# Attention transposes moved from TensorE to VectorE and SBUF-to-SBUF DMAs

## The chip, the cores and the metric

The kernel runs on one core of one Trainium2 chip. A core has a matrix engine (TensorE, PE in the profile, with its weight loads listed as PEld), a vector engine (VectorE, DVE), a scalar engine (ScalarE, ACT), a general engine (GpSimd, POOL), and SyncE (SP), which here only issues DMAs. Each engine works through its own instruction list in order; a DMA is issued from the list of SP, ACT or POOL and then runs on 16 shared DMA engines. Work is held in SBUF, and TensorE writes its results to PSUM, which has eight banks; both have 128 partitions.

The metric is the device time of one execution in microseconds. The time before is the median of three runs.

## The reference

Everything is float32. The input x has 4 batch elements of 512 rows and 1024 columns. It is layer-normed, goes through an attention branch s and a gate branch g, and the output is x + s * g.

```
xn = layernorm(x)                                # 4 x 512 x 1024
q = rmsnorm(xn @ Wq.T, q_norm_w)                 # 32 heads of 128
k = rmsnorm(xn @ Wk.T, k_norm_w)                 # 8 KV heads of 128
v = xn @ Wv.T                                    # 8 KV heads of 128
scores = q @ k.T / sqrt(128)                     # 4 query heads share a KV head
bias = where(rel > 0, -1e30, slope[head] * rel)  # rel = key position - query position
s = (softmax(scores + bias) @ v) @ Wo.T
g = silu(xn @ W.T + bias + lora(xn))             # 8 adapters of rank 16, averaged with weights
out = x + s * g
```

The mask is causal: a query looks only at keys at or before its own position.

## The kernel before

The kernel has three stages. The first layer-norms x, turns it so that its 1024 columns lie on the partitions, stores it to DRAM as the seven left operands of a Strassen product, and computes half of the gate. The last multiplies by Wo and adds everything up. The change is in the middle stage, which computes attention.

The middle stage goes through 32 units. A unit is one KV head with its four query heads (`g`, 8 values) and one batch element (`b`, 4 values, the inner loop). For each unit `project_qkv` computes queries, keys and values, 128 rows by 768 columns a tile, by two Strassen halves of seven products each (`strassen`, L118). A product is four matmuls of 384 columns (L125). Its left operand `a` is loaded from DRAM by SP just ahead of it (L384) into one of eight buffers. Banks of PSUM are saved by ScalarE (L214) and added up by VectorE (L221, L223) into the tiles `c`, one for each 128 rows. Then `norm` takes a finished tile: POOL copies v out (L398), ScalarE squares queries and keys (L400), VectorE reduces (L402) and scales (L404), POOL takes the power -1/2 (L406), VectorE multiplies (L408). `transposes` turns the 128x128 blocks of four query heads and one key head on TensorE (L420, L425), and VectorE copies them out of PSUM with the norm weights applied (L421, L426).

`attend` goes through the unit's 16 items, a head `h` and a block `i` of 128 queries. `scores` makes one tile of 128 queries by (i+1)*128 keys (L445). VectorE adds the slope times the relative position, with the mask in it (L452), and finds the negated maximum of each row (L461). ScalarE takes the exponential with its row sum (L464), VectorE forms the reciprocal (L468) and scales the row (L469). `turn` transposes the probabilities on TensorE, i+1 blocks of 128x128 (L478), and ScalarE copies them to `pt` (L479). `values` multiplies with v for one head (L487), ScalarE copies the result (L495) and issues four DMAs to DRAM (L497).

PSUM: three banks hold products, two scores, two transposes, one values.

The unit loop (L555 to L561) takes one step of the next unit's projection after each step of `attend`, so that the products stand between the score tiles on TensorE. In the last unit half of the gate for batch element 0 stands in for the projection; its products have 256 columns. The order written in the loop is not the final one: a scheduler places the instructions of each engine by its own estimates of when operands are ready, with the tile pools' buffers as limits. What counts for an engine is its final list.

## Time and profile before

The columns of the table are busy times of one profiled execution.

| | us |
|---|---|
| median of three runs (3116.28 to 3120.14) | 3118.26 |
| span of the profiled execution, first to last instruction | 3112.8 |
| device time of the profiled execution | not listed beside its span |
| TensorE busy in the span | 2969.5 (95%) |
| VectorE busy | 1622.0 (52%) |
| ScalarE busy | 835.7 (27%) |
| GpSimd busy | 560.8 (18%) |
| matmuls of the score tiles (L445) | 360.0 |
| matmuls that transpose probabilities (L478) | 225.5 |
| matmuls of values (L487) | 300.6 |
| matmuls that transpose queries and keys (L420, L425) | 81.3 and 35.8 |

One float32 matmul stands as two records in the profile. The mean duration of a group is that of single records, which overlap on TensorE; the time that a matmul holds the engine is seen better in the start times of the timeline. A row of the cost groups gives the line, engine and operation, what is written and read, the count, then busy time and mean, then the idle time just before them and what ended it. In the rows of DMA issues the last number is the median time from issue to landing.

### The profile page before, as it was taken

To read this page: it belongs to the slowest core of one execution; us is meant where nothing else is said; L and a number is where in the kernel's file an instruction comes from. 1 tells how busy PE (TensorE), PEld (TensorE's weight loads), DVE (VectorE), ACT (ScalarE), POOL (GpSimd) and SP (SyncE) were. 2 spreads that over 40 slices of the span, in tenths; PEclk is the share of its full clock that TensorE was granted. 3 is DMA by queue.
4 is the path that set the end of the run, shared out by engine and by line. 5 is a ranking of instruction groups with operands and counts; after the bars stand their busy time and mean duration, and the time that the engine had idled before them with its cause. 6 is when DMAs were issued, how large, how long until landed. Compare 5 with 4: busy or idle time off the path is not lost.

```text
span 3112.8 us, 30258 instructions
## 1 busy us (share of the span) xinstructions
PE 2969.5 (95%) x10408; PEld 1754.6 (56%) x10408; DVE 1622.0 (52%) x3474; ACT 835.7 (27%) x2132; POOL 560.8 (18%) x513
## 2 busy tenths in 40 slices
PE   7999999999999999999999999999979999999997
PEld 5766566655656556655665565656844444344443
DVE  5236665666565665666566656566332232322564
ACT  1123333333333333333333333333200000000010
POOL 5321200121020120121012102012020121311311
PEclk9999999999999999999999999999999999999999
DMA  8532332232232232233223223222662244443364
GB/s 307 206 122 78 95 89 78 78 112 75 78 113 77 75 113 78 78 90 97 78 78 112 74 78 102 75 75 82 198 230 81 108 142 138 159 142 132 134 220 148
DMA packets 201769, 360.12 MB, mean 116 GB/s; under 512 B 21520, under 2 KB 95248, under 8 KB 199056
## 3 DMA queue, kind: packets, MB, share of 16 engines
q1 hardware_dynamic: 114272, 265.86, 27.4%
q10 hardware_dynamic: 75568, 50.37, 5.1%
q0 software_dynamic: 11776, 41.95, 3.3%
q8 instruction: 84, 1.38, 0.2%
q14 instruction: 69, 0.57, 0.1%
HBM read 265.82 MB, written 92.27 MB: 115 GB/s over the span
## 4 chain that ended last, share of the span: by engine, by line
PE 82%; DVE 9%; POOL 4%; issue 2%; DMA 2%; ACT 1%; ACTq 0%; POOLq 0%; SPq 0%; DVEq 0%
PE c_p L125 20%; PE u_p L125 14%; PE c_o L125 13%; PE u_o L125 10%; PE sc L445 8%; PE ov L487 7%; PE ptp L478 4%; PE c_f L125 3%; POOL inv L406 2%; PE u_f L125 2%; PE tq L420 2%; DVE qn L408 1%; DVE pr L469 1%; DVE ss L402 1%; DVE sc L452 1%
## 5 line engine op out<-in xcount | busy, mean ns | idle before, releaser
L445 PE MATMUL sc<-kT,qT 128*128 128x128 f32 (+3 forms) x1024 | 360.0, 437 | 12.9 <-ACT pr L464 12.5
L464 ACT ACTIVATE pr<-sc,nmax 128x128 f32<-128x128 f32 (+3 forms) x512 | 269.8, 527 | 379.2 <-DVE nmax L461 321.7
L125 PE MATMUL c_p<-w,a 128*128 128x384 f32 x1024 | 361.8, 487 | 0.0
L479 ACT COPY pt<-ptp 128x128 f32<-128x128 f32 (+3 forms) x512 | 216.0, 422 | 532.0 <-PE ptp L478 527.5
L125 PE MATMUL u_p<-t_q,a 128*128 128x384 f32 x1024 | 351.6, 487 | 0.0
L125 PE MATMUL c_p<-t_q,a 128*128 128x384 f32 x1024 | 351.5, 487 | 0.0
L452 DVE SCALAR_TENSOR_TENSOR sc<-rel,sc 128x128 f32<-128x128 f32 (+3 forms) x512 | 251.5, 491 | 152.3 <-PE sc L445 145.1
L487 PE MATMUL ov<-pt,v 128*128 128x512 f32 (+3 forms) x1024 | 300.6, 433 | 0.0
L398 POOL COPY v<-c_p 128x128 f32<-128x128 f32 x128 | 37.8, 295 | 1358.8 <-DVE c_p L221 1116.1
L445 PEld LDWEIGHTS sc<-kT,qT 128*128 128x128 f32 x1024 | 182.0, 191 | 131.7 <-ACT pr L464 36.9
L461 DVE TENSOR_REDUCE nmax<-sc 128x1 f32<-128x128 f32 (+3 forms) x512 | 249.4, 487 | 11.0
L125 PE MATMUL u_o<-t_o,s 128*128 128x512 f32 x512 | 237.3, 608 | 18.2 <-DVE k_o L642 17.3
L650 DVE TENSOR_TENSOR c<-c_o,k_o 128x512 f32<-128x512 f32 x96 | 66.2, 690 | 361.4 <-ACT k_o L640 191.0
L487 PEld LDWEIGHTS ov<-pt,v 128*128 128x128 f32 x1024 | 187.3, 191 | 115.6 <-issue 50.6
L125 PEld LDWEIGHTS u_p<-t_q,a 128*128 128x128 f32 x1024 | 185.1, 191 | 107.8 <-issue 5.5
L469 DVE TENSOR_SCALAR pr<-pr,rden 128x128 f32<-128x128 f32 (+3 forms) x512 | 236.5, 462 | 13.4
L125 PEld LDWEIGHTS c_p<-t_q,a 128*128 128x128 f32 x1024 | 185.2, 191 | 102.2
L468 DVE RECIPROCAL rden<-den 128x1 f32<-128x1 f32 x512 | 83.4, 163 | 287.7 <-ACT pr L464 287.4
L478 PEld LDWEIGHTS ptp<-ident,pr 128*128 128x128 f32 x1280 | 163.0, 141 | 119.6 <-DVE qT L421 39.5
L125 PEld LDWEIGHTS c_p<-w,a 128*128 128x128 f32 x1024 | 180.5, 191 | 86.5
L478 PE MATMUL ptp<-ident,pr 128*128 128x128 f32 x1280 | 225.5, 275 | 0.0
L640 ACT COPY k_o<-u_o 128x512 f32<-128x512 f32 x48 | 28.1, 585 | 662.2 <-PE u_o L125 662.2
(110 smaller groups left out, 3645.6 us busy)
## 6 DMA issues: line engine op xcount, KB each, us to landing
a<-xs SPq DMA_DIRECT2D x448, 256.0 KB, 2.7
ot<-oh ACTq DMA_DIRECT2D x512, 64.0 KB, 1.7
o<-ot SPq DMA_DIRECT2D x64, 512.0 KB, 3.2
sums<-c POOLq DMA_DIRECT2D x48, 512.0 KB, 5.0
old<-sums SPq DMA_DIRECT2D x48, 512.0 KB, 4.0
w<-in_wq_dram SPq DMA_DIRECT2D x8, 2048.0 KB, 8.6
wo<-in_wo_dram SPq DMA_DIRECT2D x8, 2048.0 KB, 8.7
xs<-a ACTq DMA_DIRECT2D x8, 1792.0 KB, 6.7
```

The lines of the kernel that those rows point to most:

```text
L125: nc.tensor.matmul(acc, lhsT=left[k], rhs=right[k], start=start and k == 0, stop=k == nk - 1, skip_group_check=True,)
L406: nc.gpsimd.tensor_tensor(inv, ms, neg_half, ALU.pow)
L445: nc.tensor.matmul(sc[:, :w], lhsT=qT[:, h, i * P : (i + 1) * P], rhs=kT[:, :w], start=True, stop=True,)
L452: nc.vector.scalar_tensor_tensor(sc[:, :w], rel[:, S - w :], slopes[g * G + h], sc[:, :w], ALU.mult, ALU.add,)
L461: nc.vector.tensor_reduce(nmax, sc[:, :w], AX.X, ALU.max, negate=True)
L464: nc.scalar.activation(pr[:, :w], sc[:, :w], AF.Exp, bias=nmax, accum_out=den)
L468: nc.vector.reciprocal(rden, den)
L469: nc.vector.tensor_scalar(pr[:, :w], pr[:, :w], rden, None, ALU.mult)
L478: nc.tensor.transpose(tp[:, j, :], pr[:, j * P : (j + 1) * P], ident)
L479: nc.scalar.copy(pts[h][:, 0 : i + 1, i * P : (i + 1) * P], tp[:, 0 : i + 1, :])
L487: nc.tensor.matmul(ov[:, j * P :], lhsT=v[:, j, :], rhs=pt[:, j, j * P :], start=j == 0, stop=j == NT - 1,)
L650: nc.vector.tensor_tensor(dst, acc, kept, ALU.add)
```

## The change

TensorE no longer transposes anything in the middle stage. A 128x128 transpose becomes two steps: VectorE transposes each 32x32 block in its place, and DMAs from SBUF to SBUF move the blocks to the partitions where they belong.

For queries and keys, `norm` multiplies in place in `c` and transposes 128x640 elements by blocks into `flat` (one instruction a tile). When all four tiles of the unit are done, 16 DMAs on SP move `flat` to `qkT`, each from 32 partitions to 32 partitions, in pieces of 640 bytes. Both norm weights and the factor 1/sqrt(128) are joined in `w_sb` and applied to the keys alone, by one VectorE instruction (`kT`).

A score tile now holds 32 queries of all four heads, 128 rows in all, so one tile c of 16 covers 32(c+1) keys, 128 at the least. The bias of each head lies on that head's 32 partitions: a tile `bias`, 608 columns, is made once for each KV head from `rel` and `drop`, and the tile's window of it is added. The addition and the row's maximum come from one instruction, which writes the negated sum and keeps its minimum; the exponential takes scale -1. ScalarE, not VectorE, scales the rows by the reciprocal, four tiles at a time. VectorE then transposes the 32x32 blocks into `turned`, whose blocks above the diagonal are set to zero once. At the end of the unit 16 DMAs on SP move `turned` to `pt`, in pieces of 512 bytes.

`values` goes by blocks of 128 queries with all four heads in one matmul of 512 columns; it is called one unit later, while the projection after next begins. ScalarE issues one DMA for each block. PSUM: three banks for products, three for scores, two for values. `left` has six buffers in place of eight.

```
+    nc.gpsimd.tensor_scalar(drop, drop, shift, None, ALU.add)
+    nc.gpsimd.tensor_scalar(rel, drop, 0.0, slope0, ALU.min, ALU.mult)
+    nc.gpsimd.tensor_scalar(drop, drop, 0.0, MASKED, ALU.is_gt, ALU.mult)
...
-        ps_sc = front.enter_context(tc.tile_pool(name="ps_sc", bufs=2, space=PSUM))
-        ps_tp = front.enter_context(tc.tile_pool(name="ps_tp", bufs=2, space=PSUM))
-        ps_ov = front.enter_context(tc.tile_pool(name="ps_ov", bufs=1, space=PSUM))
+        ps_sc = front.enter_context(tc.tile_pool(name="ps_sc", bufs=3, space=PSUM))
...
+            turned = keep.tile([P, 4 * npairs, NT, 32], F32, name="turned")
+            for i in range(1, NT):
+                for t in range(NT - 1):
+                    c0 = 4 * (first_pair[i] + i)
+                    nc.gpsimd.memset(turned[:, c0 + t + 1 : c0 + NT, t, :], 0.0)
...
                     nc.vector.tensor_tensor(
+                        qk, qk, inv.unsqueeze(2).to_broadcast([P, G + 1, HD]), ALU.mult
+                    )
+                    nc.vector.transpose(
+                        flat[:, t], qk.rearrange("p h (a e) -> p a h e", a=4)
+                    )
+
+                yield from project(f"p_{u}", b, G + 2, stream(u, b), right, norm)
+
+                qkT = unit.tile([P, NT, 4, G + 1, 32], F32, tag="qkT", name=f"qkT_{u}", bufs=1)
+                for a in range(4):
+                    for r in range(4):
+                        nc.sync.dma_start(
+                            out=qkT[32 * a : 32 * a + 32, :, r].rearrange("p t h e -> p t (h e)"),
+                            in_=flat[32 * r : 32 * r + 32, :, a].rearrange("p t h e -> p t (h e)"),
+                        )
+                kT = unit.tile([P, 4 * NT, 32], F32, tag="kT", name=f"kT_{u}", bufs=1)
+                nc.vector.tensor_scalar(
+                    kT,
+                    qkT.rearrange("p t r h e -> p (t r) h e")[:, :, G, :],
+                    w_sb,
+                    None,
+                    ALU.mult,
+                )
...
+                def scores(i, t, den):
+                    c = 4 * i + t
+                    w = max(32 * (c + 1), P)
...
+                        lhsT=qkT[:, i, t, 0:G, :].rearrange("p h e -> p (h e)"),
...
+                    nc.vector.tensor_tensor_reduce(
+                        out=sc[:, :w],
+                        in0=sc[:, :w],
+                        in1=bias[:, at : at + w],
+                        scale=-1.0,
+                        scalar=3.0e38,
+                        op0=ALU.add,
+                        op1=ALU.min,
+                        accum_out=low,
+                    )
...
+                for i in range(NT):
+                    den = small.tile([P, NT], F32, tag="den", name=f"den_{u}_{i}")
+                    prs = []
+                    for t in range(NT):
+                        prs.append(scores(i, t, den))
+                        if t % 2:
+                            yield
+                    rden = small.tile([P, NT], F32, tag="rden", name=f"rden_{u}_{i}")
                     nc.vector.reciprocal(rden, den)
+                    for t in range(NT):
+                        c = 4 * i + t
+                        n = max(c + 1, 4)
+                        pr = prs[t][:, : 32 * n]
+                        nc.scalar.activation(pr, pr, AF.Copy, scale=rden[:, t : t + 1])
+                        c0 = 4 * first_pair[i]
+                        nc.vector.transpose(
+                            turned[:, c0 : c0 + n, t, :],
+                            pr.rearrange("p (n e) -> p n e", n=n),
+                        )
+                pt = unit.tile([P, npairs, G, P], F32, tag="pt", name=f"pt_{u}", bufs=1)
+                src = turned.rearrange("p (n m) t e -> p n m (t e)", m=4)
+                for h in range(G):
+                    for m in range(4):
+                        nc.sync.dma_start(
+                            out=pt[32 * m : 32 * m + 32, :, h, :],
+                            in_=src[32 * h : 32 * h + 32, :, m, :],
+                        )
+                held["pt"] = pt
+
+            def values(u, g, b, held):
+                pt, v = held["pt"], held["v"]
+                for i in range(NT):
+                    ov = ps_ov.tile([P, S], F32, tag="ov", name=f"ov_{u}_{i}")
                     for j in range(i + 1):
                         nc.tensor.matmul(
+                            ov,
                             lhsT=v[:, j, :],
+                            rhs=pt[:, first_pair[i] + j].rearrange("p h q -> p (h q)"),
                             start=j == 0,
+                            stop=j == i,
                         )
+                    oh = unit.tile([P, G, P], F32, tag="oh", name=f"oh_{u}_{i}")
+                    nc.scalar.copy(oh, ov.rearrange("p (h q) -> p h q", h=G))
+                    nc.scalar.dma_start(
+                        out=ot[b][g // 2][i][:, (g % 2) * G : (g % 2 + 1) * G, :], in_=oh
+                    )
                     yield
...
-            apool = mid.enter_context(tc.tile_pool(name="left", bufs=8))
+            apool = mid.enter_context(tc.tile_pool(name="left", bufs=6))
...
+            def bias_of(g):
+                bias = unit.tile([P, SPAN], F32, tag="bias", name=f"bias_{g}", bufs=1)
+                nc.vector.scalar_tensor_tensor(
+                    bias, rel, slopes[g * G] / slopes[0], drop, ALU.mult, ALU.add
+                )
+                return bias
...
+            before = None
             for n, (g, b) in enumerate(units):
+                if b == 0:
+                    bias = bias_of(g)
                 fill = start_project(*units[n + 1]) if n + 1 < len(units) else last_gate(0)
+                if before is not None:
+                    for _ in values(f"{before[0]}_{before[1]}", *before, held.pop(before)):
+                        next(fill, None)
+                for _ in attend(f"{g}_{b}", g, b, held[g, b], bias):
                     next(fill, None)
                 for _ in fill:
                     pass
...
+                before = g, b
+            fill = last_gate(1)
+            for _ in values(f"{before[0]}_{before[1]}", *before, held.pop(before)):
+                next(fill, None)
```

## The prediction

> **What bounds the kernel now.** I read the page's first part, then busy times by stretch, the cost groups, the timeline of one attention stretch, and the DMA issues.
>
> ```profile
> PE 2969.5 (95%) x10408; PEld 1754.6 (56%) x10408; DVE 1622.0 (52%) x3474; ACT 835.7 (27%) x2132; POOL 560.8 (18%) x513
> ...
> 1000.00:1600.00 600.00, 580.59 (x2249) 361.24 (x2248) 368.25 (x882) 223.77 (x591) 84.19 (x84) 0.99 0.29 86
> ...
> L478 PE MATMUL ptp<-ident,pr 128*128 128x128 f32 x1280 | 225.5, 275 | 0.0
> ...
> L406 POOL TENSOR_TENSOR inv<-ms,neg_half 128x5 f32<-128x5 f32 x128 | 152.8, 1194 | 254.8 <-DVE ms L404 254.8
> L408 DVE TENSOR_TENSOR qn<-c_p,inv 128x640 f32<-128x640 f32 x128 | 105.6, 825 | 103.2 <-POOL inv L406 103.2
> L402 DVE TENSOR_REDUCE ss<-sq 128x5 f32<-128x640 f32 x128 | 104.3, 815 | 5.2 <-ACT sq L400 1.2
> ```
>
> TensorE is the bound: busy 581 of 600 us, clock 0.99. VectorE has 368 (61%), ScalarE 224. From 400 to 2200 us L487 left 921 of its 1024 records, 32 to a unit (one KV head group, one batch element): 28.8 units, 62.5 us each, with 55.1 us of TensorE idle in all, 1.9 a unit. The 275 ns of a transpose overlap their neighbours; the timeline has the real price.
>
> ```profile
> 188.00 2.74 PE L125 MATMUL u_p<-t_q,a 128*128 128x384 f32 x8
> 190.58 0.60 PE L420 MATMUL tq<-ident,qn 128*128 128x128 f32 x4
> 191.02 0.27 PE L425 MATMUL tk<-ident,qn 128*128 128x128 f32 x1
> 191.13 2.75 PE L125 MATMUL c_p<-t_q,a 128*128 128x384 f32 x8
> ...
> 1005.12 1.78 ACTq L497 DMA_DIRECT2D ot<-oh  x4
> ```
>
> By starts, a product of 4x384 columns takes 2.58 us (1.68 ns a column) and five transposes 0.55 (0.11 each). Issuing a DMA holds its queue 0.445 us.
>
> ```profile
> ot<-oh ACTq DMA_DIRECT2D x512, 64.0 KB, 1.7
> ...
> row<-in_x_dram SPq DMA_DIRECT2D x16, 512.0 KB, 5.6
> ...
> q1 hardware_dynamic: 114272, 265.86, 27.4%
> q10 hardware_dynamic: 75568, 50.37, 5.1%
> ```
>
> The 16 engines are some 30% busy. A q1 packet averages 119 ns for 2.3 KB, about 105 ns for 2 KB. Of q10's 75568 packets 65536 are the 512-byte ones of L497; taking the rest at 105 ns from 2540 us of engine time leaves 23 ns for each.
>
> **What goes.** Per unit, 60 TensorE transposes (40 of probabilities, 16 of queries, 4 of keys): 60 x 0.11 = 6.6 us. Score columns fall from 5120 to 4544, since a tile of 32 queries and 4 heads stops at 32(c+1) keys: 576 x 1.68 ns = 1.0. Value columns stay 5120 (8.6 us). All of it lies on the bound: TensorE work falls from 60.6 to 53.0 us a unit.
>
> VectorE loses the separate reduce, the rescaling and the copies of transposed queries and keys; it gains 16 stream transposes of 128 to 512 elements and 4 of 640. No row has one. Ends: the plain rate of a VectorE pass (0.69 us at 512, 0.82 at 640) or half that rate (1.4, 1.6). I take the plain rate, the nearest rows in shape; faster would only widen slack. The fused add-and-min costs the 0.70 us of L452 at 512, plus an accumulator read between zero and the 0.19 ScalarE's takes; I take 0.16, a one-element VectorE instruction. Sum of VectorE 33 us a unit, of ScalarE 27 (16 Exp, 16 scaled copies, squares, saves): both under 53, so what matters is order.
>
> At nothing I cost: ot's 4 issues a unit in place of 16 (5.3 us off ScalarE's queue, which waits on TensorE today; a stall would gain at most these); the bias per head group (one VectorE pass of 608, 0.8 us in four units, ahead of the first tile); the POOL work at the start (three passes of 608, some 1.5 us each by L652's 1.3 at 512, and the memsets of turned, 9 of at most 0.3), beside the opening loads and gate products; if uncovered, some 7 us once.
>
> **What is added on the path.** At a unit's end SP issues 16 pt DMAs (5120 pieces of 512 bytes, 2.6 MB), then 16 qkT DMAs (2048 pieces of 640 bytes, 1.3 MB). The instruction order of the changed kernel has on TensorE: last score tile of unit n, products 12 to 14 of project(n+1), products 1 to 4 of project(n+2), values(n), scores of n+1. On SP: loads for those four products, pt(n), qkT(n+1), load 5. So pt is covered by seven products, 18.1 us.
>
> Pt chain, from the end of the last score tile: add-and-min 0.86, exp 0.69 with its sum's read 0.19, reciprocal 0.16, and 0.2 between them, 2.1; on ScalarE two scaled copies (0.5 each, L479's 0.48 at 384 and 0.58 at 512 as guide), the save of product 12's bank that stands there (0.48), two copies more (0.6 each); the last stream transpose 0.69; with 0.1 between engines pt is issued from 5.7. Sixteen issues take 7.1. The transfer's low end is 5120 x 23 ns / 16 engines = 7.3 us. Its high end, each DMA landing before the next: 16 x 1.7 = 27. I take 12: nearer the packet row, whose pieces have the same size, but above it, as each DMA reads and writes only 32 of the 128 partitions, which no row here shows. Landing 5.7 + 12 + 1.7 = 19.4, so TensorE stands 1.3 us before values.
>
> [...]
>
> QkT chain: product 14 ends at 7.7; put 8.4; square 9.2; reduce, scale 10.3; POOL's power (1.2) 11.6; multiply 12.5; then for the second tile, VectorE being in order, reduce 13.3, first transpose 14.2, scale, power 15.7, multiply 16.6, transpose 17.5. SP waits until then with load 5 behind it, issues until 24.7, lands 26.8, and the kT multiply ends at 27.6. Values end at 19.4 + 8.6 = 28.0: hidden, by 0.4 us only. Load 5 lands about 28 (2.7 after its issue), also in time. If pt landed early, this chain would hold scores until 27.6 against 26.7 of work: 0.9 stays.
>
> A second place: norm of the first half sits on VectorE between tiles 7 and 8. From the end of product 7: put, tiles 6 and 7 to 1.85, two reduces (0.82), two multiplies (0.83, each behind a 1.2 power), two 0.83 transposes and four small ones to 11.1, tile 8's add-and-min 11.7, its exp 12.4. TensorE meanwhile does tiles 6 to 10, products 8 and 9 and half of 10 and is at tile 11 by 8.9, where it needs the bank of tile 8 (three banks): 3.5 us of stall. Were the scheduler's slack better than this reckoning, zero; with half-rate transposes, 6.
>
> **Sum.** 53.0 + 1.3 + 3.5 + 0.5 for the small waits of today = 58.3 a unit, 4.2 less; over 31 units 130. Once: the first unit's 16 tiles have only 2¼ products among them, so VectorE and ScalarE (about 22 us) outlast TensorE's 13: +9. In the last two units gate products of 1.73 us stand in: three of 2.58 and four of 1.73 cover 14.7 us of the 19.4, nine of 1.73 cover 15.6; beyond the usual 1.3 that is 3.4 and 2.5, and with a shorter middle of the last unit +9. Net 130 - 18 = 112. The profiled execution's span is 3112.8; no device time is listed for it, the median of the three runs is 3118.3, and I carry the 5.5 between them along. 3118 - 112 = 3006, called **3010 us**.
>
> [...]
>
> **Rivals.** (a) *The likeliest*, as summed, 2950 to 3080.
> (b) *Slower: the partition-crossing transfer outlasts its cover.* Without the pt stall a unit would gain 5.5; 5.5 x 31 - 18 = 152, or 4.9 us of stall a unit, is break-even: a pt transfer of 15.6 us. At 20 us the stall is 9.3 and qkT, queued behind, lands 2.1 after values: 53 + 11.4 + 4 = 68.4, 3118 + 31 x 5.9 + 18 = 3320. At 27, values start at 34.4 and end at 43.0, kT comes at 48.6: 79 a unit, about 3650. For it: 7168 small pieces a unit on one queue, two hops through 32 partitions; against it: 23 ns packets and engines 70% idle.
> (c) *All hidden.* Transfer 7.3, no wait in the middle: 53 + 0.9 + 0.5 = 54.4, 3118 - 31 x 8.1 + 18 = 2885. For it: the packet row; against it: VectorE's serial norm.
> (d) *Half-rate stream transposes.* Middle wait 6; pt chain +0.7, so values end at 28.7; qkT chain +2.4, so kT comes at 30.0; boundary 2.0 + 1.3: 53 + 3.3 + 6 + 0.5 = 62.8, 3118 + 31 x 0.3 + 18 = 3145.
> That the transposes don't leave TensorE is excluded: its instruction list has none at those lines.
>
> **Chances.** (a) 0.47, (b) 0.28, (c) 0.13, (d) 0.12. Changes within 0.2% (6 us) cannot be told from none. Faster: (c) and nearly all of (a), 0.58; same 0.03; slower 0.39. The range leaves out the far part of (b), above 20 us of transfer, and the fastest of (c): 2900 to 3320.
>
> **What would show it.** Right: TensorE busy falls by about 240 us, the unit's period is 58, waits on pt of 1 to 3 us before L516's matmuls, waits of sc on ScalarE's exp of 3 us before tile 11, pt landing 14 us after its first issue. Wrong: pt taking over 16 us from first issue to last landing; stream transposes above 1 us at 640; kT or the loads behind qkT holding scores; score tiles waiting on VectorE all along a unit.

## The result, and the profile after

The changed kernel takes 3148.4 us (3145.2 to 3153.3), the kernel before 3118.3: a ratio of 1.0096, 95% interval 1.0082 to 1.0110. It is slower by 1%; 3010 us had been forecast. The profiled execution spans 3151.5 us against 3112.8, 38.7 more.

The page of the changed kernel: busy time, the granted clock in 40 slices, the queue that SP's DMAs go through, the chain that ended last, two groups of matmuls, and the two new moves among the DMA issues.

```profile
PE 2826.4 (90%) x8104; PEld 1551.5 (49%) x8104; DVE 1315.5 (42%) x3003; ACT 838.2 (27%) x2132; POOL 562.3 (18%) x532
...
PEclk9999999999999989999999999998989999999999
...
q1 hardware_dynamic: 360032, 391.75, 44.8%
...
PE 52%; SPq 16%; DVE 13%; POOL 7%; DMA 6%; issue 3%; ACT 3%; ACTq 0%; POOLq 0%; DVEq 0%
...
L516 PE MATMUL ov<-pt,v 128*128 128x512 f32 x640 | 356.3, 722 | 151.7 <-DMA qkT<-flat 116.1
L456 PE MATMUL sc<-kT,qkT 128*128 128x128 f32 (+12 forms) x1024 | 311.8, 424 | 78.8 <-ACT pr L476 63.8
...
pt<-turned SPq DMA_DIRECT2D x512, 160.0 KB, 3.8
qkT<-flat SPq DMA_DIRECT2D x512, 80.0 KB, 2.4
```

TensorE is busy 143 us less, not 240. Nearly all of the difference lies in matmuls that took longer than before: `ov` has 356.3 us where 32 times 8.75, its length without a wait, makes 280, and the products from `t_q` into `u_p` have 377.1 in place of 351.6. A new bound took the rest of the gain: SP's queue has 16% of the chain that ended last. Idle time of 151.7 us stands ahead of the `values` matmuls (L516). The name in its bracket, qkT, is only the landing that the profile saw last; what those matmuls wait for is pt, whose last copies SP issues just before qkT's first (in the boundary below pt's last copy lands at 1045.72, and `ov` starts at 1045.92). ScalarE's exponentials hold up the score tiles for 63.8 us, 2 us a unit.

The same stretch as before, 1000 to 1600 us: the columns are the stretch, its length, busy time of TensorE, its weight loads, VectorE, ScalarE and POOL, then the granted clock, the DMA engines' share and GB/s.

```profile
1000.00:1600.00 600.00, 534.30 (x1556) 299.05 (x1555) 278.25 (x748) 227.78 (x603) 82.54 (x84) 0.94 0.54 144
```

TensorE's 581 us have become 534, VectorE's 368 have become 278, and the granted clock has fallen from 0.99 to 0.94. One boundary between two units, from the last score tile of one to the first of the next, tells the story. This is the timeline of the changed kernel; the columns are start, length, engine, line, operation, and in brackets the idle time ahead of it. The last score tile ends at 1023.34 (21.51 and 1.83).

```profile
1021.51 1.83 PE L456 MATMUL sc<-kT,qkT 128*128 128x480 f32 x4
1028.74 14.02 SPq L505 DMA_DIRECT2D pt<-turned  x16
1038.65 2.74 PE L128 MATMUL c_p<-t_q,a 128*128 128x384 f32 x8
1039.76 0.83 DVE L424 STREAM_TRANSPOSE flat<-c_p 128x640 f32<-128x640 f32 x1
1042.85 11.61 SPq L433 DMA_DIRECT2D qkT<-flat  x16
1045.92 10.24 PE L516 MATMUL ov<-pt,v 128*128 128x512 f32 x20 [4.52 <-DMA qkT<-flat]
1056.63 0.49 DVE L438 TENSOR_SCALAR kT<-qkT,w_sb 128x512 f32<-128x512 f32 x1 [16.03 <-DMA qkT<-flat]
1057.17 0.71 PE L456 MATMUL sc<-kT,qkT 128*128 128x128 f32 x4 [1.01 <-DVE kT L438]
```

SP begins to issue pt 5.4 us after the last score tile and needs 14.0 us for 16 copies. The seventh product ends at 1041.4; `ov` can start only 4.5 us later. `flat` was complete at 1040.6, but SP comes to qkT 2.3 us after that, and needs another 11.6 us.

`ov` itself takes 10.24 us, where 8.75 is its length without a wait. The granted clock shows why; the columns are those of the stretch above.

```profile
1020.00:1045.30 25.30, 21.40 (x66) 12.06 (x64) 12.12 (x25) 7.96 (x18) 2.92 (x4) 1.00 0.59 128
1045.40:1048.70 3.30, 2.78 (x4) 1.26 (x5) 0.00 (x0) 0.59 (x1) 0.00 (x0) 0.50 0.59 127
1048.80:1056.00 7.20, 7.20 (x18) 2.94 (x16) 0.00 (x0) 1.17 (x2) 0.00 (x0) 1.00 0.85 230
```

At the start of `ov` the granted clock is 0.50, for 3.41 us in all (1045.36 to 1048.77); before and after it is 1.00.

All runs below are compared by the period, the distance from the first `ov` of the first unit to the first `ov` of the 31st, divided by 30. It is 63.7 us in the changed kernel. The same reading of the kernel before gives 63.2, where the prediction, which counted records in a stretch, had 62.5. So a steady unit is 0.5 us longer than before instead of 4.2 shorter. The 38.7 us of the two profiled spans divide as follows: the middle stage's first product starts at 178.27 us, before at 164.78 (+13.5); from there to the first product of the last stage 2159.4, before 2132.5 (+26.9, of which 0.5 us a unit over 31 units make 15.5 and the ends of the middle stage the rest, 11); the last stage is 1.8 shorter.

### The profile page after: what moved, and what is told of

Read it like the earlier page. It is cut to its first block, busy times and chain, and to the rows that moved or that the text cites. A ratio compares the mean times of both kernels' runs of the same rounds, so it can differ in the third digit from the quotient of the medians.

```text
span 3151.5 us, 26438 instructions
## 1 busy us (share of the span) xinstructions
PE 2826.4 (90%) x8104; PEld 1551.5 (49%) x8104; DVE 1315.5 (42%) x3003; ACT 838.2 (27%) x2132; POOL 562.3 (18%) x532
## 3 DMA queue, kind: packets, MB, share of 16 engines
q1 hardware_dynamic: 360032, 391.75, 44.8%
## 4 chain that ended last, share of the span: by engine, by line
PE 52%; SPq 16%; DVE 13%; POOL 7%; DMA 6%; issue 3%; ACT 3%; ACTq 0%; POOLq 0%; DVEq 0%
PE c_o L128 13%; SPq L505 11%; PE u_o L128 10%; PE c_p L128 9%; PE sc L456 6%; PE ov L516 6%; SPq L433 5%; PE u_p L128 5%; DVE turned L497 3%; POOL inv L420 3%; PE c_f L128 2%; DMA qkT<-flat 2%; DVE c_p L421 2%; PE u_f L128 2%; DVE flat L424 2%
## 5 line engine op out<-in xcount | busy, mean ns | idle before, releaser
L516 PE MATMUL ov<-pt,v 128*128 128x512 f32 x640 | 356.3, 722 | 151.7 <-DMA qkT<-flat 116.1
L456 PE MATMUL sc<-kT,qkT 128*128 128x128 f32 (+12 forms) x1024 | 311.8, 424 | 78.8 <-ACT pr L476 63.8
L128 PE MATMUL u_p<-t_q,a 128*128 128x384 f32 x1024 | 377.1, 508 | 2.5 <-DMA a<-xs 2.2
L476 ACT ACTIVATE pr<-sc,low 128x128 f32<-128x128 f32 (+12 forms) x512 | 251.5, 493 | 341.2 <-DVE low L465 333.1
L516 PEld LDWEIGHTS ov<-pt,v 128*128 128x128 f32 x640 | 147.1, 236 | 353.6 <-issue 329.6
L465 DVE CUSTOM_DVE_ANT_0 sc<-sc,bias 128x128 f32<-128x128 f32 (+12 forms) x512 | 225.6, 459 | 212.9 <-PE sc L456 208.7
L456 PEld LDWEIGHTS sc<-kT,qkT 128*128 128x128 f32 x1024 | 186.2, 199 | 213.9 <-ACT pr L476 91.2
L128 PEld LDWEIGHTS u_p<-t_q,a 128*128 128x128 f32 x1024 | 199.2, 197 | 144.4 <-issue 29.9
L128 PE MATMUL u_o<-t_o,s 128*128 128x512 f32 x512 | 236.3, 605 | 17.5 <-DVE k_o L676 17.3
L495 ACT ACTIVATE pr<-pr,rden 128x128 f32<-128x128 f32 (+12 forms) x512 | 236.5, 522 | 15.9 <-DVE rden L490 15.9
L497 DVE STREAM_TRANSPOSE turned<-pr 128x128 f32<-128x128 f32 (+12 forms) x512 | 218.3, 456 | 38.2 <-ACT pr L495 38.2
L524 ACT COPY oh<-ov 128x512 f32<-128x512 f32 x128 | 75.0, 586 | 514.9 <-PE ov L516 486.5
L674 ACT COPY k_o<-u_o 128x512 f32<-128x512 f32 x48 | 28.1, 586 | 660.2 <-PE u_o L128 660.2
L420 POOL TENSOR_TENSOR inv<-ms,neg_half 128x5 f32<-128x5 f32 x128 | 149.5, 1168 | 253.1 <-DVE ms L418 199.5
L128 PE MATMUL u_p<-w,a 128*128 128x384 f32 x512 | 175.6, 486 | 0.0
```

Source lines behind the costliest of these rows:

```text
L128: nc.tensor.matmul(acc, lhsT=left[k], rhs=right[k], start=start and k == 0, stop=k == nk - 1, skip_group_check=True,)
L420: nc.gpsimd.tensor_tensor(inv, ms, neg_half, ALU.pow)
L456: nc.tensor.matmul(sc[:, :w], lhsT=qkT[:, i, t, 0:G, :].rearrange("p h e -> p (h e)"), rhs=kT[:, :w], start=True, stop=True,)
L465: nc.vector.tensor_tensor_reduce(out=sc[:, :w], in0=sc[:, :w], in1=bias[:, at : at + w], scale=-1.0, scalar=3.0e38, op0=ALU.add, op1=ALU.m ...
L476: nc.scalar.activation(pr[:, :w], sc[:, :w], AF.Exp, bias=low, scale=-1.0, accum_out=den[:, t : t + 1],)
L495: nc.scalar.activation(pr, pr, AF.Copy, scale=rden[:, t : t + 1])
```

## The experiments

Theory A says that the 32 copies of a unit cost more than forecast where they are issued, on one queue, one after the other, and that TensorE waits for them. Its variants and rivals stand in each expectation. Cover is the work that TensorE has to do while copies run. All experiments but two fix the order of TensorE's instructions in a unit, so that the scheduler's own choices can't change with the edit. The control for that stands first here but was run after most of the others, so the first of their expectations start from 3148 us, the changed kernel's time.

**The control: the order alone.**

```diff
+                if k == 0 and "ov" in last:
+                    behind(mm, last["ov"])
...
+                        if i == 0:
+                            behind(mm, last["mm"])
...
+                    if c == 0 and "ov" in last:
+                        behind(mm, last["ov"])
+                    if c == 1:
+                        last["ov"] = mm
...
+                    for _ in range(4):
+                        next(fill, None)
                     for _ in values(f"{before[0]}_{before[1]}", *before, held.pop(before)):
-                        next(fill, None)
+                        pass
```

`behind` puts an instruction after another on TensorE: products after the last `ov` or the second score tile, the first `ov` after the fourth product, the first score tile after the last `ov`.

> A control, nothing left out: the changed kernel with the order of TensorE's instructions in the middle stage fixed as it already is (four products, values, scores), as all the other experiments but that with the late w_sb have it. 3143 to 3153 us, if the way of writing the order changes nothing; outside it, the experiments must be read against this run.

Measured 3189.8 us, ratio 1.0226 (1.0211 to 1.0242): outside. The period is 63.3, against 63.7, and the parts of a unit are the changed kernel's within 0.2 us; so the 41 us are not in the steady units. The profiled spans stand 36 us apart: the first `ov` comes 36 us later, the 30 periods behind it give 12 back, and the last units lose as much again. The first score tile and the first `ov` of the control's timeline:

```profile
235.36 1.22 PE L471 MATMUL sc<-kT,qkT 128*128 128x128 f32 x4 [22.20 <-DVE kT L453]
...
315.20 8.75 PE L535 MATMUL ov<-pt,v 128*128 128x512 f32 x20
```

In the changed kernel the first `ov` starts at 279.25. My edit put the second unit's products behind the second score tile of the first unit as well, where no `values` stand ahead; TensorE then waits 22 us with nothing to do. The times of the experiments with a fixed order are therefore read against 3189.8 us, and their periods, which the opening does not touch, against 63.3.

**No moves at all.**

```diff
-                qkT = unit.tile([P, NT, 4, G + 1, 32], F32, tag="qkT", name=f"qkT_{u}", bufs=1)
-                for a in range(4):
-                    for r in range(4):
-                        nc.sync.dma_start(
...
+                qkT = flat
...
-                for h in range(G):
-                    for m in range(4):
-                        nc.sync.dma_start(
...
-                            rhs=pt[:, first_pair[i] + j].rearrange("p h q -> p (h q)"),
+                            rhs=turned[:, 4 * (first_pair[i] + j) : 4 * (first_pair[i] + j) + 4].rearrange("p n t e -> p (n t e)"),
```

> Left out: both moves between partitions. values take turned and scores take flat directly (flat in two buffers), so the output is not attention; every matmul, every pass of VectorE, ScalarE and POOL stays, and TensorE's order of a unit is that of the changed kernel. Theory A (the 32 copies of a unit, and what waits for them, ate the gain): the 4.5 us before ov, the 1.0 us before the first score tile and ov's extra 1.6 us all go, the 2.1 us before tile 11 stays; period 62.4 - 7 = 55.4, 3148 - 31 x 7 = 2930 us (2900 to 2970), clock back near 0.98. Rival B (the clock is low for another reason than the waits, say the new mixture of work): TensorE stays busy 55.3 a unit at 0.94 and the time is 2990 to 3030. Rival C (VectorE's and ScalarE's order in the middle of a unit is as much of a bound as the copies): waits before tiles 8 to 15 grow, over 3050 us.

Measured 2873.9 us, ratio 0.9212 (0.9199 to 0.9224), period 54.9. The stretch from 1000 to 1600 us, and the boundary: the last score tile ends at 976.32, kT is ready 17.8 us later, `ov` follows the seventh product without a wait and takes 8.75 us.

```profile
1000.00:1600.00 600.00, 576.72 (x1796) 332.00 (x1795) 319.59 (x850) 257.98 (x681) 104.91 (x100) 1.00 0.33 102
```

```profile
993.62 0.48 DVE L447 TENSOR_SCALAR kT<-flat,w_sb 128x512 f32<-128x512 f32 x1
994.22 8.75 PE L520 MATMUL ov<-turned,v 128*128 128x512 f32 x20
1002.80 0.61 PE L465 MATMUL sc<-kT,flat 128*128 128x128 f32 x4
```

Theory A's cause holds and B and C fall: without the moves the clock is back (1.00 in this stretch, 0.984 over the run), and the period is shorter than the control's by 8.4 us. The time is 26 us below A's range all the same: its sum started from a unit of 62.4 us and took 7 away, where 63.7 became 54.9. All else in the change is worth 244 us against the kernel before. The moves cost 274 us against the changed kernel, whose first `ov` comes as early as this run's (279.25 and 278.88); of the 316 against the control 36 lie ahead of the first `ov`.

**Half the bytes of pt.**

```diff
-                            out=pt[32 * m : 32 * m + 32, :, h, :],
-                            in_=src[32 * h : 32 * h + 32, :, m, :],
+                            out=pt[32 * m : 32 * m + 32, : npairs // 2, h, :],
+                            in_=src[32 * h : 32 * h + 32, : npairs // 2, m, :],
```

> Left out: five of the ten blocks of pt; values read the other five twice. 16 copies a unit as before, each 80 KB in place of 160. Theory A1 (SP's issue of a copy has a floor of its own, some 0.6 us, as the first of 16 took and as qkT's of 80 KB took): the 16 issues take 9 to 10 us in place of 14.0, SP comes to qkT at 17.5, its 16 issues end at 27, scores wait for kT until 30: period 59, 3045 us (3030 to 3080), and the wait before the score tiles is now 3 us. Rival A2 (bytes alone set the pace, 180 GB/s in both halves): the 16 issues take 7.0 us, 0.44 each, qkT's 8 us at most; period 57, below 3010 us.

Measured 3104.3 us, ratio 0.9951 (0.9935 to 0.9968), period 61.6. From its timeline:

```profile
1074.77 10.29 SPq L524 DMA_DIRECT2D pt<-turned  x16
...
1094.71 10.37 SPq L448 DMA_DIRECT2D qkT<-flat  x16
...
1095.32 8.75 PE L535 MATMUL ov<-pt,v 128*128 128x512 f32 x20
...
1108.20 1.23 PE L471 MATMUL sc<-kT,qkT 128*128 128x128 f32 x4 [4.13 <-DVE kT L453]
```

Half the bytes do not take half the time: a copy of 80 KB takes 0.66 us of SP from start to start, one of 160 KB had taken 0.88. The two fit a floor (A1), and above it something that goes with the size. The wait ahead of `ov` is gone and `ov` is at 8.75 us again; but qkT, which SP can begin only when `flat` is ready, now ends last, and the score tiles wait 4.7 us on average. The time is 59 us above the 3045 expected. That figure had been taken off 3148, not off the control, and of the 3.4 us a unit that A1 counted on only 1.7 came: the wait for kT is longer than the 3 us expected, and the score part grew by 0.7.

**qkT from POOL's queue.**

```diff
                     for r in range(4):
-                        nc.sync.dma_start(
+                        nc.gpsimd.dma_start(
```

> Nothing left out: qkT's 16 copies are issued by POOL's queue, pt's stay on SP; TensorE's order is unchanged. Theory A1 (the queue that issues is the limit, and qkT waits behind pt on it): qkT starts at 17.3 us after the last score tile in place of 19.5 and takes 9 us beside pt's tail, kT is ready under ov, the 1.0 us before the first score tile goes and loads of a come earlier: 3148 - 31 x 1.1 = 3114 us (3100 to 3130). Rival A2 (the two share a limit on bytes between groups of 32 partitions): pt's last landings come later by what qkT takes from them, the wait before ov grows past 4.5 us, 3148 us or more. Rival A3 (POOL needs more than 1 us for such a copy): kT comes later than now, waits of scores of 3 us and more, 3200 us or over.

Measured 3255.4 us, ratio 1.0434 (1.0419 to 1.0450), period 66.0: slower, against what A1 expected.

```profile
1141.66 6.05 POOL L448 DMA_DIRECT2D qkT<-flat  x11 [2.67 <-DVE flat L439]
...
1148.37 11.24 PE L535 MATMUL ov<-pt,v 128*128 128x512 f32 x20 [6.51 <-issue]
...
1149.37 0.55 POOL L448 DMA_DIRECT2D qkT<-flat  x1 [1.66 <-DMA qkT<-flat]
```

POOL issues eleven copies at 0.55 us each and then stops, each time until an earlier one has landed; landing takes 6.4 us (median) in place of 2.4. The program has each of these copies wait for the one eight ahead of it: over 30 units the last five copies start 0.28 us (median) after that one has landed. SP's issues of pt are as before (0.88 us), but `ov` starts 23.8 us after the last score tile, 1.2 later than in the control: with qkT's copies under way at the same time `ov` had to wait longer for pt, as A2 said. Both chains got later; kT is ready 36.8 us after the last score tile.

**The late w_sb** (this one without a fixed order).

```diff
-            nc.vector.tensor_scalar(
-                w_sb, qw_sb, kw_sb, 1.0 / math.sqrt(HD), ALU.mult, ALU.mult
-            )
             nc.vector.tensor_scalar(coef, coef, LORA_SCALE, None, ALU.mult)
...
-            a_of[0, 1] = layernorm(0, 1)
+            a_of[0, 1], scaled = layernorm(0, 1)
+            product_w = nc.vector.tensor_scalar(
+                w_sb, qw_sb, kw_sb, 1.0 / math.sqrt(HD), ALU.mult, ALU.mult
+            )
+            tc.add_manual_dep(
+                product_w.ins,
+                scaled.ins.name,
...
```

> Nothing left out: the product w_sb of the two norm weights is put behind the rows' first passes on VectorE, so that the scaling of lb_sb no longer stands behind the wait for kw_sb. If that wait is what delays the opening by 13.5 us: the first pl matmul starts at 12 us in place of 18.7, the middle stage's first product at 165 to 171 in place of 178.3, 3135 to 3142 us. If POOL's three passes over 608 columns (6.4 us, ahead of the powers) are the cause: pl starts early but the middle stage still at 175 to 178, 3145 to 3148 us.

Measured 3144.9 us, ratio 1.0077 (1.0064 to 1.0091): 3.6 us less than the changed kernel, a difference that the intervals hardly separate. The opening shows it better. The changed kernel:

```profile
16.88 0.21 DVE L283 TENSOR_SCALAR w_sb<-qw_sb,kw_sb 128x1 f32<-128x1 f32 x1 [8.24 <-DMA kw_sb<-in_kw_dram]
...
18.70 5.46 PE L300 MATMUL pl<-lb_sb,laT 128*128 128x512 f32 x6 [12.54 <-DVE lb_sb L287]
```

and the kernel with the late w_sb:

```profile
11.79 5.26 PE L297 MATMUL pl<-lb_sb,laT 128*128 128x512 f32 x6 [5.67 <-DVE lb_sb L284]
...
170.33 2.74 PE L128 MATMUL u_p<-w,a 128*128 128x384 f32 x8
```

One instruction on one column waited 8.2 us for `kw_sb`, and the scaling of `lb_sb` stood behind it. Without that the middle stage starts 7.9 us earlier, and still 5.5 later than before; the expectation named 165 to 171 us for its start, and 3135 to 3142 us, which was not reached, for the time. Those 5.5 lie in the opening too; that they are POOL's passes was not tried.

**Long pieces.** `turned` becomes [128, 4, 10, 4, 32] and `pt` [128, 4, 10, 128], `flat` and `qkT` likewise, so that a copy takes one run of memory from each partition.

```diff
-                            out=pt[32 * m : 32 * m + 32, :, h, :],
-                            in_=src[32 * h : 32 * h + 32, :, m, :],
+                            out=pt[32 * m : 32 * m + 32, h].rearrange("p n x -> p (n x)"),
+                            in_=turned[32 * h : 32 * h + 32, m].rearrange("p n t e -> p (n t e)"),
```

> Nothing left out: the same 32 copies with the same bytes between the same groups of 32 partitions, but the tiles are laid out so that a copy takes one run of 5120 bytes from a partition (pt) or 2560 (qkT) in place of ten of 512 or four of 640; nine more, smaller stream transposes a unit. Theory A1 (the cost of a copy goes by its number of pieces: 320 pieces 0.88 us, 160 pieces 0.66, 128 pieces 0.65): some 0.4 us an issue, pt lands at 5.7 + 9 + 2 = 17 us after the last score tile, under the products; qkT, issued from 17.5, lands at 26 and kT is there by 26.6; nothing waits at the boundary, period 55.5, 2890 us (2870 to 2930). Rival A2 (32 partitions at a time carry no more than some 180 GB/s, whatever the pieces): pt's issues stay at 0.88 us, ov waits 4 to 5 us as now, 3130 to 3160 us. In between, pieces and partitions each a part: 2950 to 3100.

Measured 3116.3 us, ratio 0.9992 (0.9983 to 1.0001), period 61.1. The page's row of SP's queue, and the boundary:

```profile
q1 hardware_dynamic: 163424, 391.75, 44.5%
```

```profile
1521.14 11.92 SPq L527 DMA_DIRECT2D pt<-turned  x16
...
1536.11 8.82 PE L538 MATMUL ov<-pt,v 128*128 128x512 f32 x20 [2.48 <-DMA qkT<-flat]
```

Neither theory as it stood: 0.75 us an issue of pt. With 45% of the packets the same bytes keep the DMA engines busy for nearly the same share (44.5% against 44.8%), so these pieces are not what the engines' time goes by. qkT's issues hardly changed (0.70 to 0.67 us).

**pt's copies in another order.**

```diff
-                for h in range(G):
-                    for m in range(4):
+                for d in range(4):
+                    for h in range(G):
+                        m = (h + d) % 4
```

> Nothing left out: the 16 copies of pt in another order, so that of two copies after each other neither the source nor the target group of 32 partitions is the same (now four copies in a row read the same group). If a group's own access is the limit (rival A2 in its form of ports that are shared by neighbours in the queue): an issue falls below 0.75 us, the wait before ov to 2 us or less, 3148 - 31 x 3 = 3055 us or less. If pieces, or the whole queue, set the pace: 0.88 us as now and 3140 to 3155 us.

Measured 3135.7 us, ratio 1.0052 (1.0035 to 1.0069), period 61.7, 0.75 us an issue. It lies between the two expectations and does as much for the pace of the issues as the long pieces. That neighbours in the queue get in each other's way when they read the same 32 partitions fits 0.75 us in place of 0.88, but was not shown by itself: whether the source or the target side decides was not tried.

**More cover.** Long pieces and the rotated order together, and one product moved from among the score tiles to ahead of `values` (the edit against the control).

```diff
-                    for _ in range(4):
+                    for _ in range(5):
                         next(fill, None)
```

> Nothing left out: long pieces and the rotated order of pt together, and one product more (eight in place of seven, 20.5 us) between the last score tile and values; the score tiles keep six. Theory A (the copies take a certain time on SP's one queue, and the boundary is the longer of cover and copies): 16 issues of 0.70 us put pt's landing at 5.7 + 11.2 + 3.6 = 20.5, so no or hardly a wait before ov, ov back at 8.75 us and ending at 29.2; qkT's 16 issues run from 17.5 to 28.1, kT at 31: scores wait 1.7 us. Boundary 31 as in the run with long pieces, the score part 2.6 us shorter less what it then waits: period 59 to 60, 3050 us (3030 to 3085). Rival C (the product taken from the score tiles was needed there): the score part keeps its 30 us, period 61, 3110 us.

Measured 3045.8 us, ratio 0.9764 (0.9748 to 0.9780), period 58.8.

```profile
1419.13 10.10 SPq L528 DMA_DIRECT2D pt<-turned  x16
...
1430.85 10.06 SPq L447 DMA_DIRECT2D qkT<-flat  x16
...
1434.04 8.75 PE L539 MATMUL ov<-pt,v 128*128 128x512 f32 x20
...
1443.63 0.94 PE L470 MATMUL sc<-kT,qkT 128*128 128x128 f32 x6 [0.84 <-DVE kT L452]
```

As theory A had it, wait by wait: pt at 0.65 us an issue, no wait ahead of `ov`, and 1.7 us on average ahead of the score tiles. The score part of a unit fell from 29.6 us in the control to 28.1 when 2.6 us of product went.

**Two hardware queues for qkT**: eight copies from ScalarE's queue, placed there behind a copy that saves products; the copies of `ov` go to VectorE.

```diff
-                        nc.sync.dma_start(
+                        queue = nc.scalar if r % 2 else nc.sync
+                        move = queue.dma_start(
...
-                    nc.scalar.copy(oh, ov.rearrange("p (h q) -> p h q", h=G))
+                    moved = nc.vector.tensor_copy(oh, ov.rearrange("p (h q) -> p h q", h=G))
```

> Nothing left out: as the run with more cover, and qkT's 16 copies half on SP's queue, half on ScalarE's; the copies of ov out of PSUM go to VectorE, which has nothing else to do there. Theory A1 (one queue's issues in a row are what qkT takes): qkT is issued from 17.5 to 22.5 us on both queues, kT is ready at 26, under ov, which ends at 29.2; no wait at the boundary but a small one for pt; period 57, 2985 us (2960 to 3020), clock above 0.97. Rival A2 (the two queues share a limit on bytes): kT at 31 as with one queue, pt's landing later, 3050 us or more.

Measured 3252.5 us, ratio 1.0428 (1.0413 to 1.0444), period 65.9: the worst miss so far. The view of waits, SP's queue (what is waited for, us in total, times, longest), and the timeline:

```profile
SPq L533 <- DMA qkT<-flat: 267.0, 77, 9.8
```

```profile
1541.15 19.91 SPq L533 DMA_DIRECT2D pt<-turned  x16
...
1552.89 5.12 ACTq L450 DMA_DIRECT2D qkT<-flat  x8
```

SP's copies of pt wait for ScalarE's copies of qkT, which wait for `flat`: 8.6 us a unit, in the wrong direction. No data asks for it: the program has copies of pt wait for copies of qkT that ScalarE issues. So the run says nothing on A1 against A2; two queues have to be tried where neither waits for the other.

**Six of qkT's copies from POOL**, with more cover and the late w_sb.

```diff
-                        nc.sync.dma_start(
+                        queue = nc.gpsimd if (a + r) % 3 == 0 else nc.sync
+                        queue.dma_start(
```

> Nothing left out: as the run with more cover (3046 us), with six of qkT's 16 copies on POOL's queue, ten on SP's, and the late w_sb. Theory A1 (what is left is qkT's issues in a row on one queue): SP issues from 17.5 to 24.0 us, POOL six from 17.5 to 21; kT by 27.5, under ov, which ends at 29.2; the 1.7 us before the score tiles go, period 57.3, opening 4 us earlier: 2990 us (2975 to 3015). If copies from POOL land as late as when all 16 were there (6.4 us and more) and hold pt's last ones: kT at 29 to 31, 3030 to 3060 us.

Measured 2947.4 us, ratio 0.9457 (0.9434 to 0.9480), period 56.0.

```profile
1363.90 6.41 SPq L456 DMA_DIRECT2D qkT<-flat  x10
1364.43 3.01 POOL L456 DMA_DIRECT2D qkT<-flat  x6 [2.64 <-DMA pt<-turned]
...
1367.08 8.75 PE L548 MATMUL ov<-pt,v 128*128 128x512 f32 x20
...
1375.67 0.83 PE L479 MATMUL sc<-kT,qkT 128*128 128x128 f32 x6
```

With six on POOL's queue nothing stops there, and a copy from it lands in 3.1 us. kT was expected at 27.5 us after the last score tile; it is ready at 27.1 in this boundary and at 28.1 on average, under `ov`, and the score tiles wait 0.2 us on average. The time is 43 us better than expected, because the score part fell to 26.7 us as well. The clock accounts for that: a score part that has a stretch at half clock in it lasts 28.2 us with more cover and 28.0 here, one without 26.1 in both, and with more cover 25 of 27 units have such a stretch, here 8. TensorE's wait ahead of tile 11 is 2.3 us in both runs; why half clock follows it so much less often here is open.

**A sixth product ahead of values**, all copies on SP again (against the control).

```diff
-                    for _ in range(4):
+                    for _ in range(6):
                         next(fill, None)
```

> Nothing left out: as the run with more cover (3046 us), with one product more again ahead of values (nine between the last score tile and ov, five among the score tiles), all copies on SP's queue, and the late w_sb. Theory A (cover against copies): ov runs from 23.1 to 31.8 us, kT is ready at 31: no wait at the boundary; the score part falls from 28.0 by less than the 2.6 us moved, to 26.5: period 58.3, opening 4 us earlier, 3022 us (3000 to 3040). Rival C (the score tiles are bound by VectorE's and ScalarE's order with fewer products among them): the score part stays near 28, period 60, 3070 us.

Measured 3315.8 us, ratio 1.0629 (1.0613 to 1.0645), period 68.0: a miss of 290 us.

```profile
1505.26 10.11 SPq L536 DMA_DIRECT2D pt<-turned  x16
...
1519.19 10.00 SPq L455 DMA_DIRECT2D qkT<-flat  x16
1529.29 2.90 SPq L421 DMA_DIRECT2D a<-xs  x6
...
1532.35 4.88 PE L140 MATMUL c_p<-t_q,a 128*128 128x384 f32 x8 [12.05 <-DMA a<-xs]
```

The sixth product's left operand is loaded by SP, behind both moves; TensorE waits 12 us for it. The expectation had counted the cover and forgotten what stands in the queue. Neither A nor C was tested.

**One part of the change alone**, in the kernel before: bias and maximum in one VectorE instruction, transposes still on TensorE.

```diff
-                    nc.vector.scalar_tensor_tensor(
...
-                    nc.vector.tensor_reduce(nmax, sc[:, :w], AX.X, ALU.max, negate=True)
+                    nc.vector.tensor_tensor_reduce(
+                        out=sc[:, :w],
+                        in0=sc[:, :w],
+                        in1=bias[:, h, S - w :],
+                        scale=-1.0,
...
+                        accum_out=nmax,
+                    )
```

> The kernel before with one part of the change alone: bias and max in one VectorE instruction, the bias of a head ready in a tile; transposes stay on TensorE. If the gain that is there without the moves (245 us) is TensorE's transposes, VectorE's saving of some 0.6 us a tile is off the path: 3100 to 3122 us. If it is VectorE's shorter chain from a score tile to its transpose: the 1.9 us of TensorE idle a unit go, 3060 us or less.

Measured 3090.1 us, ratio 0.9911 (0.9894 to 0.9927), period 62.2 against 63.2.

```profile
PE 2949.6 (96%) x10408; PEld 1743.7 (57%) x10408; DVE 1420.5 (46%) x3506; ACT 838.2 (27%) x2132; POOL 558.0 (18%) x513
```

VectorE does 202 us less, and 28 us of it reach the end, which lies between the two ranges expected. TensorE is idle only 7 us less and busy 20 us less, at a clock of 0.990 over the run in place of 0.986; where the 20 come from was not followed. It is a small part of the 244 us. By subtraction the rest belongs to the parts of the change that were not in this run, the transposes taken from TensorE with the tile shapes that go with them; that no run shows by itself.

**The first unit set free**: the run with POOL's share, where products are held behind a unit's score tiles only once there are `values` ahead.

```diff
-                    if c == 1:
+                    if c == 1 and "ov" in last:
                         last["ov"] = mm
```

> Nothing left out: as the run with POOL's share (2947 us), but the first unit's score tiles no longer hold back the products of the second: in the runs with a fixed order the products stood behind the second score tile of the first unit also, with nothing of values ahead. If that is where the control lost 41 us (its first ov at 315.2 us in place of 279.3, its period the same): the first ov comes at 266 to 275 us in place of 302, the period stays at 56.2, and the time is 2910 us (2900 to 2925). If the first unit's chain to kT has no cover whichever way the products stand, 2940 to 2950 us.

Measured 2925.4 us, ratio 0.9383 (0.9370 to 0.9396): 6.2% faster than the kernel before, and the fastest of the versions that leave nothing out.

```profile
275.98 8.75 PE L548 MATMUL ov<-pt,v 128*128 128x512 f32 x20
```

The first `ov` starts at 275.98 us in place of 301.97, and the period is 56.1 in place of 56.0; the time is 22 us less than that of the run with POOL's share, just above the range expected.

The steady unit of the runs with pt's moves, in us. The first column is the pace of pt's issues on SP, start to start; then `ov`'s start after the last score tile, its length, the wait of the score tiles behind it, and the score part (from the first score tile to the end of the last), as means over 27 units; then how many of the 27 have half clock within the score part, and the period.

| run | pt issue | ov starts | ov lasts | wait for kT | score part | half clock | period |
|---|---|---|---|---|---|---|---|
| changed kernel | 0.88 | 22.6 | 11.1 | 0.2 | 29.7 | 17 | 63.7 |
| half bytes | 0.66 | 17.9 | 8.75 | 4.7 | 30.4 | 27 | 61.6 |
| qkT from POOL | 0.88 | 23.8 | 11.0 | 2.1 | 29.3 | 13 | 66.0 |
| long pieces | 0.75 | 20.6 | 9.9 | 0.8 | 29.9 | 23 | 61.1 |
| rotated | 0.75 | 21.5 | 10.5 | 0.2 | 29.5 | 14 | 61.7 |
| more cover | 0.65 | 20.5 | 8.75 | 1.7 | 28.1 | 25 | 58.8 |
| two hardware queues | 1.33 | 29.5 | 10.6 | 0 | 26.0 | 2 | 65.9 |
| POOL's share | 0.65 | 20.5 | 8.75 | 0.2 | 26.7 | 8 | 56.0 |
| first unit free | 0.65 | 20.5 | 8.75 | 0.2 | 26.7 | 11 | 56.1 |

## Why the prediction was wrong

**The step that failed is the chain of pt: "Sixteen issues take 7.1" and "Landing 5.7 + 12 + 1.7 = 19.4, so TensorE stands 1.3 us before values".** The sum let SP issue in 7.1 us, at 0.445 us a copy by the DMAs that ScalarE had issued for `ot`, while the transfer ran on behind it for 12 in all. But SP needs 14.0 us for pt's 16 copies, 0.88 each, and the last lands 2.9 us after that: 22.3 us after the last score tile on average, not 19.4, and TensorE stands 4.5 us, not 1.3. qkT's 16 issues take 11.2, so SP is held 25.2 us a unit, not 14.2, and is through with qkT at 30.7, not 24.7. In the changed kernel that second delay costs the score tiles only 0.2 us, because `ov` ends as late; it becomes the wait that counts (4.7 and 1.7 us) in the runs with half the bytes and with more cover. The run without moves shows that these copies are what a unit loses, and the run with more cover that their order, their pieces and the cover decide how much.

**The 0.88 us is not the price of issuing alone.** With long pieces or with another order the same bytes go out at 0.75 a copy, with both at 0.65, which makes 10.4 for sixteen. So of the 6.9 us that pt's issues took beyond 7.1, 3.3 stand at the lowest pace found and 3.6 go with pieces and order.

**What the transfer needs of the DMA engines was nearly right, what it lasts was not.** Over the whole run the moves added 245760 packets and 559 us of busy time on the 16 engines (44.8% of 3151.5 less 27.4% of 3112.8); by the two moves' shares of the 125.9 MB added, pt's 2.62 MB take 11.6 us of all engines, close to the 12 taken, which was the author's estimate between 7.3 and 27 and stood in no row of before. From pt's first issue to its last landing it is 16.9 us, though, where 13.7 had been reckoned; over 16 was one of the prediction's own signs of being wrong.

**`ov` of 8.6 us failed too, for a reason not in the prediction.** After the wait it takes 11.1 us on average, 8.75 where nothing was waited for: the half clock of the boundary above. This adds 2.5 us a unit, nearly as much as the longer wait (3.2). Both together with the kT wait make the 58.3 us of the sum into 63.5: score part, start of `ov`, `ov` were to be 30.3 (53.0 less the seven products and `ov`, and the 3.5 and 0.5 of waits), 19.4 and 8.6, and are 29.65, 22.56 and 11.07, with 0.23 for kT. That the score part came so close is in part luck: its wait was 1.4 us shorter than forecast, but in 17 of 27 units it held a stretch at half clock, and lasted 30.2 us in place of 28.7.

**Right in the sum:** pt issued from 5.7 (5.4 measured); `flat` ready at 17.5 (17.3); stream transposes at the plain rate (0.83 us for 640 columns); the fused instruction at 0.70 us for 512; the place and the engine of the wait before tile 11, though not its size (3.5 forecast, 2.1 measured); TensorE's own work, 53.0 us a unit, where the run without moves has 54.9 less 2.1 of waits. Rival (c), "all hidden", had 54.4 us a unit and 2885 us, and that run gives 54.9 and 2874; but here errors cancel, for (c) had no wait within the unit, and had 0.9 us for kT that the run hasn't.

**Costed at nothing, and wrong:** the opening. The w_sb multiply was left out of the working, and the cover named there was for POOL's passes; 13.5 us, of which the late w_sb gives 7.9 back. The ends of the middle stage were put at 18 and came to 11.

**Rival (b), a transfer that outlasts its cover, is what happened.** The forecast gave it 0.28. That its break-even fits as well, 17.3 us from pt's first issue to the last landing against 16.9 measured, with steady units within 0.5 us of before, is luck: (b) had no slow `ov`, which costs 2.5 us, it had 1.4 us more of waiting before tile 11, and it took the unit before at 62.5 us, not 63.2. Its condition could have been weighed better: the sum put the stall at 1.3 us where 4.9 would have undone the gain, and the prices of issue and transfer came from copies of other shapes.

The 138 us between forecast and result: 4.7 us a unit over 31 units (4.2 less was forecast, 0.5 more measured) are 146, the opening 13.5; the ends gave 7 back, the last stage 1.8, the profiled spans stand 8.6 further apart than the medians, and 3006 had been called 3010.

## What to carry to other kernels

A move by many small DMAs holds the queue that issues it (here 14.0 us for pt's 16 copies): multiply the count by a duration from a copy of the same shape in the same row of copies, then write down what stands behind it on that queue, in both directions, loads and the waits of one queue for another too. When a bound engine is given less work, its waits at the seams decide (here 4.5 us a unit ahead of `ov`); move cover there, and check that the cover's own operands do not come through the queue it is to hide. An experiment that fixes an order needs a run of that order alone before anything is read from it.

## What the runs showed of the hardware

**A short wait costs TensorE more than its length.** Take the first 31 units of the changed kernel and of the twelve runs made from it, 403 in all. In 188 the `ov` matmuls started after at most 0.6 us of idle time, and none took over 9.6 us. Of 29 that came after 2.3 to 3 us of idle time 19 took some 10.5 and the others 8.8; of 30 after 3.1 to 4 us 29 took over 10.2, and all 156 after more than 4 us took 10.2 to 11.9. In the boundary shown the granted clock is 0.50 for the first 2.9 us, and the weight loads beneath run at 0.34 us in place of 0.19. Over the whole execution of the changed kernel the trace has 61 stretches at 0.50, 34 of them 3.41 us long and 23 of them 6.83; before there were 15. Which wait brings one on is not shown: in some cases 2.3 us was enough.

**The pace of such copies had a floor in these runs.** In the changed kernel none of SP's took under 0.59 us, and qkT's had a median of 0.60. From start to start the lowest pace was some 0.65, for 80 KB in pieces of 512 bytes (half the bytes) and for 160 KB in pieces of 5120 (more cover); ScalarE's eight took 5.12 us, POOL's eleven 6.05 and POOL's six 3.01. Above the floor the pace followed size, pieces and order (0.88 us in the changed kernel, 0.75 with long pieces or the rotated order), and the two together brought it down to it. Loads of `a` in the same queue, 256 KB from DRAM to 128 partitions, mostly took 0.32 to 0.53 us. What makes the floor is open.

**Copies from POOL land in 3.1 us when six stand in a row and in 6.4 us when sixteen do** (medians); with sixteen POOL stopped after the eleventh, and the last five started 0.28 us (median) after the copy eight ahead had landed.
